# Reordering the hand-written issue lists of a two-layer graph network kernel

## The chip, the cores and the metric

The kernel runs on one core of one Trainium2 chip. Time is device microseconds of one execution, from the runs' own clock; the profile's span counts from the first to the last instruction of one profiled execution. All data are float32, except the masks, which are stored as bfloat16.

## The reference

There are 128 batches of 128 nodes with 512 features, x[128,128,512], and an integer adjacency adj[128,128,128]. Two layers, each with a residual and a normalisation:

```python
# layer 0: attention with 8 heads of 64
q, k, v = x @ Wq + bq, x @ Wk + bk, x @ Wv + bv
logits  = where(adj > 0, q @ k.T / sqrt(64), -1e9)
x = layernorm(x + relu(softmax(logits) @ v @ Wo + bo))
# layer 1: graph attention with one head
Wh = x @ W;  e = leaky(Wh @ a1 [:, None] + Wh @ a2 [None, :])
attention = softmax(where(adj > 0, e, -9e15), axis=1)
x = layernorm(x + leaky(attention @ Wh))
```

## The kernel before, in words

**Engines and order.** Every instruction is issued in an order that is written out. The lists BEGIN, STEADY and PLAN hold short tokens, and a token becomes the few instructions of one piece of work. Each engine (TensorE, VectorE, ScalarE, GpSimd, and SP, which issues the DMAs) works through its own pieces in the order of the list and waits at a piece until what it needs is there. Where pieces of different engines stand relative to each other in a list has no meaning of its own, beyond which buffer a piece is given.

**Stages.** BEGIN is the prologue: it loads and prepares the weights, computes group 0 (a group is four batches) directly, and starts six batches. STEADY has four lists, used for t = 6 to 123 by t % 4. An even t and the odd t after it handle the pair of batches t, t + 1. PLAN is the epilogue for the last four batches.

**Tokens of the steady lists.** `f` and `s` are the first and second batch of the pair: `scores` (TensorE, line 875, eight products of 64 rows, each in two records, into two PSUM banks), `add` (VectorE, line 889: adds the mask, one call for each bank), `reduce` (VectorE, line 898: row maxima), `exp.a.b` (ScalarE, line 909, one call and an accumulator read for each head), `reciprocals` (VectorE, 919), `divide` (ScalarE, 923), `store` and `fetch` (SP: the probabilities go through DRAM, lines 930 and 936, since the fetch reorders them in blocks of 32), `transpose` (VectorE, 942), `attend` (TensorE, 955, products into 64 columns), `copy` (ScalarE, 970), `sum` (GpSimd, 523 to 526).

`h` is a half step of the projections Q, K, V of the next group. They are computed four batches at once with two nested levels of a Strassen-Winograd scheme: seven outer products p1 to p7 (TensorE, line 681, eight records for an even chain, six for an odd one), with partial results in three PSUM banks `st_y`, `st_w`, `st_x`. `a` does the oldest copy out of PSUM that is due (ScalarE, 694), `d` the oldest addition (VectorE, 715), `k` and `k.v` the oldest combination (line 731) on GpSimd and on VectorE. `q` (SP, line 634) fetches the next projection weights into a ring of four tiles. `i.sNx` are the inner sums (line 500) of the next group's inputs, on VectorE with `.v` and else on GpSimd, `m.sum.n` the outer ones (GpSimd).

`z` is the output projection of layer 0 of the pair before, `w` layer 1's product with W: p1 to p7 (TensorE, line 801), t0, t2, t3 (copies, ScalarE, 812), c11 to c22 (VectorE: 1059, 1063, 1047 for z, 1146 for w). A copy t0 or t2 must have read bank y before p6 or p7 adds to it. `z.stats`, `n.stats` (VectorE, 1003 and 1005), `rstd` (GpSimd, 1009 and 1011), `apply` (VectorE, 1024) are the normalisations. `e` is layer 1's attention of one batch (`turn_blocks` 1187, `add` 1191, `maxima` 1197, `exp` 1201, `divide` 1205, `product` 1211, `copy` 1218, all small), `n` its residual (1221) and normalisation, `g` the store and fetch of layer 0's result for layer 1, `v` the round trip of layer 1's row terms, `m` loads, casts and transposes of the inputs.

**Banks.** PSUM has eight banks: three for the projections, five shared by scores, attention outputs and the banks y, w and x of `z` and `w`, `e.product` among them. A piece that asks for a bank waits until the last reader of the tile that held it is done.

Of the kernel before, what the change touches and what calls it, by code (L numbers as in the profile page):

```python
# [23 lines left out]
    y.order.3 y.q.0.0 y.order.2 b0.masks y.q.1.0 y.rows.2 y.rows.3 b4.load.1 b6.load.0  # L24
    b5.load.2 w.bias b2.masks y.q.2.0 y.q.2.1 y.q.1.1 y.oq.1 y.k.3 y.k.1 y.k.2 b4.turn
    b1.cast y.q.3.0 y.q.0.1 b0.cast y.oq.2 b7.load.1 y.q.3.1 b1.mask wk.build.0 b6.turn
    b5.turn wk.build.1 b3.cast b0.mask wk.build.2 wk.build.3 y.ok.2 b2.cast wq.scale.0
    y.oq.0 wq.scale.1 wq.scale.2 y.ok.1 y.ok.3 wq.scale.3 wk.build.4 wk.build.5 y.k.0 y.ok.0
    y.oq.3 s0.scores wk.build.6 b7.turn wk.build.7 b2.mask b3.mask s1.scores g1.0 g1.2
    b9.load.0 b8.load.2 w.halve wq.build.0 wq.build.1 wk.store.0 wq.build.2 s0.add.1  # L30
    s0.add.0 g1.1 i1.s1b b4.masks s0.reduce s1.add.0 s1.add.1 i1.s2b g1.3 wk.store.1
    s0.exp.0.1 s0.exp.6.7 b4.cast s0.exp.4.5 i1.s1a.v wk.store.2 y.v.1 wk.store.3 s0.exp.2.3
    b5.cast q q y.v.0 y.v.2 y.v.3 i1.s3a.v s1.reduce wq.build.4 s0.reciprocals.0
    s0.reciprocals.1 s0.divide.4.5 s0.divide.2.3 i1.s2a wq.build.3 i1.s4a.v wq.build.5
    s1.exp.5.6 s0.divide.0.1 h s1.exp.7 s1.exp.3.4 s0.divide.6.7 y.ov.0 s1.exp.0.1 y.ov.2
# [133 lines left out]
def kernel(  # L169
# [155 lines left out]
    wk = Weights(late)  # L325
# [702 lines left out]
    class LayerZero:  # L1028
# [727 lines left out]
```

## Time and profile before

| | us |
|---|---|
| median of 3 runs | 2305.35 (2304.18 to 2306.50) |
| the profiled execution | 2304.29 |
| its span | 2302.5 |
| granted TensorE clock | 0.998 |

The costliest groups of the page have means of 397 ns for each exponential and each division (ScalarE, 1000 of each), 1189 ns for a row maximum and 1236 ns for the transpose of a batch's probabilities (VectorE, 125 of each), 776 ns for the application of a normalisation (VectorE, 239), and about 275 ns for a projection product and 390 for one of `z` or `w` (TensorE). Matmuls overlap, so these last durations are not what one costs: the distance between two starts is. A "record" is one row of the trace; each float32 product is two of them.

Steady work repeats every four batches: the wait of the second attention product, for example, comes at 1046.67 us and at 1117.08 us, some 70.4 us apart.

### The profile page before, as it was taken

How to read it: one execution, taken by the hardware profiler on the slowest of the kernel's cores; microseconds unless marked ns; L12 is line 12 of the kernel's file. 1: busy time of each engine (PE TensorE's matmuls, PEld its weight loads, DVE VectorE, ACT ScalarE, POOL GpSimd, SP SyncE). 2: the span in 40 equal slices, each digit the busy share in tenths (PEclk: the TensorE clock that was granted, in tenths of full speed). 3: DMA queues.
4: the chain of work that ended last, by engine and by line, in shares of the span. 5: the costliest groups of instructions: out<-in, count | busy, mean ns of one | idle time of the engine just before them, and what ended most of it. 6: DMA issues, size and time to landing. Idle time of an engine off the chain costs nothing.

```text
span 2302.5 us, 52596 instructions
## 1 busy us (share of the span) xinstructions
PE 2265.1 (98%) x17228; PEld 2013.5 (87%) x17228; DVE 2076.6 (90%) x4199; ACT 1661.2 (72%) x5955; POOL 1443.9 (63%) x1723
## 2 busy tenths in 40 slices
PE   9899999999999999999999999999999999999998
PEld 5889888888898898888988988889889889888885
DVE  5889999999999999999999999999999999999977
ACT  3767767777677677776776776877767767768786
POOL 2666676666766666666667666666666676666656
PEclk9999999999999999999999999999999999999999
DMA  9988888878888888888878888788888788888764
GB/s 234 278 232 233 235 236 243 243 233 228 242 234 251 235 230 237 242 243 239 234 228 243 233 246 241 233 233 242 242 240 237 225 246 235 247 236 233 214 214 144
DMA packets 516593, 540.79 MB, mean 235 GB/s; under 512 B 100568, under 2 KB 394336, under 8 KB 516320
## 3 DMA queue, kind: packets, MB, share of 16 engines
q1 hardware_dynamic: 516000, 537.17, 80.3%
q8 instruction: 137, 2.24, 0.4%
q14 instruction: 136, 1.11, 0.2%
q10 hardware_dynamic: 320, 0.26, 0.0%
HBM read 388.96 MB, written 148.31 MB: 233 GB/s over the span
## 4 chain that ended last, share of the span: by engine, by line
PE 58%; DVE 19%; DMA 9%; POOL 6%; SPq 3%; issue 3%; ACT 2%; DVEq 0%; POOLq 0%; ACTq 0%
PE p_y L801 14%; PE st_y L681 13%; PE lg L875 6%; PE p_w L801 6%; PE st_w L681 6%; PE st_x L681 5%; DVE pa L942 4%; PE p_x L801 4%; DMA w_n<-wv 3%; PE p_oT L955 3%; DVE arena L1047 3%; DVE cells L715 2%; DVE st L1003 2%; PE p_h L1211 2%; DVE arena L1024 2%
## 5 line engine op out<-in xcount | busy, mean ns | idle before, releaser
L909 ACT ACTIVATE pa<-pa,nmax 128x128 f32<-128x128 f32 x1000 | 391.6, 397 | 8.7 <-DVE nmax L898 8.7
L923 ACT ACTIVATE pa<-pa,rs 128x128 f32<-128x128 f32 x1000 | 329.2, 397 | 14.4 <-DVE rs L919 14.3
L1009 POOL TENSOR_SCALAR ve<-mv 128x1 f32<-128x1 f32 x256 | 77.6, 303 | 289.5 <-DVE mv L1005 228.4
L694 ACT COPY cells<-st_y 128x384 f32<-128x384 f32 x279 | 131.7, 472 | 101.4 <-PE st_y L681 98.9
L1024 DVE TENSOR_SCALAR arena<-arena,mv,rstd 128x512 f32<-128x512 f32 x239 | 185.5, 776 | 14.3 <-POOL rstd L1011 14.1
L909 ACT ACTIVATION_READ_ACCUMULATOR pa<-pa,nmax 128x1 f32 x1000 | 194.6, 195 | 0.0
L970 ACT ACTIVATE arena<-p_oT,b_cols 128x128 f32<-128x128 f32 x504 | 144.1, 371 | 58.9 <-PE p_oT L955 54.8
L523 POOL TENSOR_TENSOR x1S<-x1T 128x256 f32<-128x256 f32 x62 | 57.6, 929 | 204.2 <-DVE mf L853 204.2
L1011 POOL TENSOR_TENSOR rstd<-ve,mhalf 128x1 f32<-128x1 f32 x256 | 160.8, 628 | 21.3
L1003 DVE BATCH_NORM_STATS2 st<-arena 128x6 f32<-128x512 f32 x248 | 168.0, 678 | 1.2
L889 DVE TENSOR_TENSOR pa<-lg,mf 128x512 f32<-128x512 f32 x250 | 161.2, 675 | 4.6 <-PE lg L875 4.6
L942 DVE STREAM_TRANSPOSE pa<-paz 128x1024 f32<-128x1024 f32 x125 | 154.5, 1236 | 8.5 <-DMA paz<-pa_dram 6.1
L955 PE MATMUL p_oT<-pa,out_V 128*64 128x128 f32 x2000 | 136.9, 279 | 16.8 <-DVE pa L942 16.8
L875 PEld LDWEIGHTS lg<-out_K,out_Q 64*128 64x128 f32 x2048 | 125.0, 188 | 32.4 <-issue 20.4
L875 PE MATMUL lg<-out_K,out_Q 64*128 64x128 f32 x2048 | 149.4, 286 | 0.7 <-ACT out_K L1395 0.7
L694 ACT COPY out_V<-st_y 128x512 f32<-128x512 f32 x124 | 72.1, 581 | 106.7 <-PE st_y L681 106.5
L898 DVE TENSOR_REDUCE nmax<-pa 128x8 f32<-128x1024 f32 x125 | 148.6, 1189 | 0.1
L955 PEld LDWEIGHTS p_oT<-pa,out_V 128*64 128x64 f32 x2000 | 106.7, 136 | 40.0 <-DVE pa L942 31.2
L1218 ACT ACTIVATE arena<-p_h 128x512 f32<-128x512 f32 x120 | 71.5, 596 | 87.8 <-DMA out_dram<-arena 60.5
L801 PE MATMUL p_y<-wo_w,x1S 128*128 128x257 f32 x496 | 134.3, 393 | 0.2
L801 PE MATMUL p_y<-wo_w,x1T 128*128 128x257 f32 x496 | 132.0, 388 | 0.0
L801 PE MATMUL p_y<-wo_w,oS 128*128 128x256 f32 x504 | 129.8, 380 | 0.4 <-ACT y L812 0.4
(301 smaller groups left out, 7851.7 us busy)
## 6 DMA issues: line engine op xcount, KB each, us to landing
paz<-pa_dram SPq DMA_DIRECT2D x504, 128.0 KB, 3.5
pa_dram<-pa SPq DMA_DIRECT2D x125, 512.0 KB, 3.7
w_n<-wk SPq DMA_DIRECT2D x93, 512.0 KB, 5.5
w_n<-wv SPq DMA_DIRECT2D x93, 512.0 KB, 5.1
w_n<-wk SPq DMA_DIRECT2D x93, 384.0 KB, 4.3
w_n<-wv SPq DMA_DIRECT2D x93, 384.0 KB, 5.0
x_dram<-arena SPq DMA_DIRECT2D x128, 256.0 KB, 2.8
xz<-x_dram SPq DMA_DIRECT2D x240, 128.0 KB, 4.1
```

Of the source, the lines that this page charges most:

```text
L681: nc.tensor.matmul(p[:, index, :], lhs, rhs, start=start and index == 0, stop=True, skip_group_check=True,)
L694: nc.scalar.copy(dst, p)
L801: nc.tensor.matmul(p[:, :width], xs()[n][:, kc, :], w[:, PLACE[n], kc, :], start=start and kc == 0, stop=True, skip_group_check=True,)
L875: nc.tensor.matmul(self.lg[r][:, c, :], q[rows, 2 * (b % 2) + c % 2, c // 2, :], k[rows, 2 * (b % 2) + c % 2, c // 2, :], start=c == 0, st ...
L889: nc.vector.tensor_add(by_head[:, r * NC : (r + 1) * NC], self.lg[r].rearrange("p c (b k) -> p c b k", b=4), mf.unsqueeze(1).to_broadcast( ...
L909: nc.scalar.activation(self.pa[:, :, h, :], self.pa[:, :, h, :], AF.Exp, bias=self.nmax[:, h : h + 1], accum_out=self.sums[:, h : h + 1],)
L923: nc.scalar.activation(self.pa[:, :, h, :], self.pa[:, :, h, :], AF.Copy, scale=self.rs[:, h : h + 1])
L942: nc.vector.transpose(self.paT.rearrange("p h (a i) -> p a h i", i=32), self.paz.rearrange("p a (h k) -> p a h k", k=32),)
L955: nc.tensor.matmul(self.oT[r * HD : (r + 1) * HD, c, :], v[:, c % 2, c // 2, r * HD : (r + 1) * HD], self.paT[:, r * NC + c, :], start=c == 0,
L1003: nc.vector.bn_stats(st, self.src)
L1011: nc.gpsimd.tensor_tensor(self.r, ve, mhalf, ALU.pow)
L1024: nc.vector.tensor_scalar(self.src, self.src, self.mv[:, 0:1], self.r, ALU.subtract, ALU.mult)
```

## The change

All three lists are written anew, with the same pieces of work in them. In STEADY:

- `s.scores` follows `f.scores` with no other TensorE piece between them (t % 4 = 0 and 2); before, two half steps and `w.p1`, or `w.p1`, stood there.
- In t % 4 = 1 `z.apply.1` comes behind `s.transpose` and the addition `d` ahead of it (before: `z.apply.1`, `s.transpose`, `z.stats.0`, `d`); `s.add`, `s.exp` and `s.divide` move between lists (`s.exp.5`, `s.exp.6.7`, `s.reciprocals.1`); the `w` products, the half steps, `e` and `n` stand in new orders.
- Inner sums: s1b goes to VectorE, s2b and s3b to GpSimd; of the 24 combinations of a group VectorE does 10 in place of 11.
- SP: `f.fetch` moves from t % 4 = 1 to the end of 0; `q`, `s.store`, `s.fetch` stand at new places.

BEGIN moves `s2.scores` and `s3.scores` forward, has three inner sums of group 1 on GpSimd in place of VectorE (and one the other way), and loads and prepares weights in another order. PLAN puts `s1.scores` behind `s0.scores` and `s3.attend` behind `s2.attend`. One function changes: the norms of a pair are made one at a time.

```diff
 BEGIN = """
...
-    b5.cast q q y.v.0 y.v.2 y.v.3 i1.s3a.v s1.reduce wq.build.4 s0.reciprocals.0
-    s0.reciprocals.1 s0.divide.4.5 s0.divide.2.3 i1.s2a wq.build.3 i1.s4a.v wq.build.5
-    s1.exp.5.6 s0.divide.0.1 h s1.exp.7 s1.exp.3.4 s0.divide.6.7 y.ov.0 s1.exp.0.1 y.ov.2
-    y.ov.1 z0.bw s1.exp.2 b10.load.1 w.w1_load.6 w.load i1.s4b.v a w.w1_load.5 w.w1_load.2
-    w.w1_load.3 q h s2.scores h h i1.s3b.v b4.mask wq.build.7 wq.build.6 y.ov.3 a h q
...
-    d s2.reduce b9.turn d h wv.build.5 s2.exp.6.7 s2.exp.2.3 a s1.divide.2.3 wv.store.0 h
-    s3.scores h s2.exp.0.1 z0.by a h wv.store.2 wv.build.6 wv.build.7 s2.exp.4.5
-    s0.transpose s2.reciprocals.0 b11.turn a s2.divide.2.3 b7.cast d b10.turn h s0.attend
...
+    s1.add.0 s1.add.1 g1.3 i1.s1a i1.s2a i1.s3a wk.store.3 b10.load.1 q q w.load y.v.1
+    s1.reduce i1.s4a s0.reduce wq.build.2 b2.mask w.halve wq.build.3 wq.build.4 b3.mask
+    i1.s1b.v i1.s2b y.v.0 y.v.2 y.v.3 s1.exp.3.4 s0.exp.4.5 y.ov.1 b5.cast s1.exp.7
...
+    z0.by s0.divide.6.7 s0.divide.4.5 y.ov.0 y.ov.3 s2.scores h wv.build.1 wv.build.2 h
...
+    s3.scores h h a s1.divide.6.7 w.w1_load.0 b11.load.2 q h h s0.fetch b10.turn s2.add.0 d
+    s2.reduce d b9.turn b7.cast s2.exp.4.5 s0.transpose b4.mask a s2.exp.0.1 a s2.exp.6.7
+    wv.build.3 wv.build.4 h h s0.attend h h d wv.store.2 wv.store.0 wv.build.5 s1.store
...
 """

 STEADY = {
     0: """
-        k.v n.residual q f.scores h h m.masks m.sum.0 m.sum.1 m.sum.2 m.sum.3 k.v g.apply.0
-        q k.v w.p1 f.add.0 f.add.1 g.store.0 e.turn_blocks a e.add m.cast w.t0 s.scores
-        f.reduce w.p6 f.exp.0.1 f.exp.2.3 d w.t2 f.exp.4.5 f.exp.6.7 d n.stats s.add.0
-        f.reciprocals.0 s.add.1 e.maxima f.reciprocals.1 s.reduce w.p5 h n.rstd w.p7 w.p2 h
-        h m.residuals q g.fetch_both a w.t3 e.exp q q w.c22 w.c11 f.divide.2.3 s.exp.2
-        f.divide.0.1 a f.divide.6.7 e.divide w.p4 w.p3 h h h w.c21 s.exp.5 v.senders
-        f.divide.4.5 s.exp.0.1 a i.s1a.v n.apply d s.exp.6.7 s.exp.3.4 q n.store v.store
-        f.store g.transpose.1 g.transpose.0 i.s3a.v e.product h m.x_pair i.s2a i.s1b m.turn
-        d k.v m.mask i.s3b.v a s.reciprocals.0 s.reciprocals.1 w.c12 d i.s2b.v k.v e.copy
-        v.fetch
+        f.scores m.sum.0 m.sum.2 e.turn_blocks k.v m.sum.1 k.v g.apply.0 n.residual f.add.1
+        f.add.0 s.scores q w.p1 h e.add f.reduce n.stats s.add.0 a w.t0 w.p6 h w.p2 m.turn d
+        e.maxima s.add.1 f.exp.2.3 w.t2 f.exp.0.1 f.exp.6.7 a f.exp.4.5 e.exp w.p7 h m.sum.3
+        s.reduce d h h f.reciprocals.0 e.divide i.s1a.v w.p5 g.store.0 m.residuals m.masks q
+        q n.rstd g.fetch_both w.t3 m.cast a f.divide.2.3 a f.divide.0.1 s.exp.0.1 q d w.c22
+        w.c11 f.reciprocals.1 w.p4 w.c21 v.senders f.divide.6.7 h w.p3 h h n.apply i.s1b.v
+        k.v g.transpose.1 m.mask g.transpose.0 n.store v.store f.divide.4.5 a s.exp.2
+        s.exp.3.4 s.exp.5 i.s2a f.store m.x_pair v.fetch f.fetch e.product h i.s2b a d
+        i.s3a.v s.reciprocals.0 w.c12 d e.copy k i.s3b
     """,
     1: """
-        p.sum.0 z.by n.residual h z.p2 h k h a s.divide.5.6 i.s4a a f.fetch z.p1 h h d
-        n.stats n.rstd k.v m.turn e.turn_blocks s.divide.3.4 s.divide.7 s.divide.0.1
-        s.divide.2 n.apply z.bw z.t0 h z.p6 z.t2 a m.cast z.p5 z.p7 k k k h z.c11
-        f.transpose z.t3 e.add d z.p4 s.store z.c22 a z.p3 h h m.mask e.maxima z.c21 s.fetch
-        n.store q e.exp a a d z.stats.1 e.divide i.s4b h e.product h f.attend z.c12 e.copy
-        f.copy p.sum.1 z.rstd.1 p.sum.2 z.apply.1 s.transpose q z.stats.0 d s.attend s.copy
-        p.sum.3 z.rstd.0 k k s.sum.2 s.sum.0 s.sum.1 k s.sum.3 m.x_one z.store.1
+        z.by s.divide.2 k.v n.residual h h h z.p1 i.s4b i.s4a a s.exp.6.7 z.t0 z.p2 z.p6 d
+        n.stats s.reciprocals.1 a s.divide.0.1 s.divide.3.4 s.divide.7 s.divide.5.6 k.v
+        e.turn_blocks m.turn z.c11 h h h s.store z.t2 e.add z.bw a e.maxima e.exp d
+        f.transpose n.rstd z.p5 z.p7 h q m.x_one s.fetch z.t3 e.divide z.c22 a m.cast z.p4
+        z.c21 n.apply n.store k h h z.p3 m.mask d h z.stats.1 z.c12 q k p.sum.0 k z.rstd.1
+        e.product h d f.attend a a e.copy q s.transpose s.attend z.stats.0 z.apply.1 f.copy
+        s.copy p.sum.2 k k p.sum.1 z.rstd.0 s.sum.0 p.sum.3 k z.store.1 s.sum.2 s.sum.1
+        s.sum.3
     """,
     2: """
-        f.scores n.residual g.apply.0 w.p1 f.add.1 f.add.0 s.scores e.turn_blocks w.t0 e.add
-        w.p6 f.reduce w.t2 w.p2 h w.p7 m.turn k.v k.v f.exp.4.5 f.exp.6.7 f.exp.0.1 k.v w.p5
-        h w.t3 a f.exp.2.3 n.stats f.reciprocals.1 w.c22 e.maxima w.c11 f.reciprocals.0
-        e.exp f.divide.2.3 n.rstd w.p4 h w.c21 v.senders a d n.apply f.divide.4.5
-        f.divide.6.7 f.divide.0.1 e.divide s.add.0 s.add.1 d h w.p3 q g.store.0 m.residuals
-        m.masks h e.product h h a a g.fetch_both m.x_one n.store v.store s.reduce
-        g.transpose.0 w.c12 q f.store v.fetch q m.cast d g.transpose.1 m.mask s.exp.5 e.copy
+        n.residual e.turn_blocks f.scores g.apply.0 f.add.0 f.add.1 s.scores w.p1 e.add w.t0
+        w.p2 w.p6 w.p5 f.reduce e.maxima k f.exp.4.5 e.exp w.t2 w.p7 f.exp.6.7 f.exp.2.3
+        w.t3 m.residuals g.store.0 q m.masks f.exp.0.1 h a h m.turn k.v n.stats e.divide
+        f.reciprocals.1 k.v m.x_one g.fetch_both s.add.1 f.divide.6.7 w.p4 n.rstd w.c21 h
+        n.apply d w.c11 m.cast h w.c22 f.reciprocals.0 v.senders a d e.product h h n.store
+        f.divide.0.1 s.add.0 w.p3 h a f.divide.4.5 s.reduce a f.divide.2.3 v.store q f.store
+        v.fetch e.copy w.c12 g.transpose.1 g.transpose.0 d m.mask
     """,
     3: """
-        s.exp.3.4 z.by s.exp.6.7 k.v n.residual n.stats p.sum.0 h f.fetch a s.exp.2 z.p2
-        z.p1 h h s.exp.0.1 z.t0 n.rstd q k.v z.p6 p.sum.1 p.sum.2 s.reciprocals.0
-        s.reciprocals.1 d s.divide.5.6 a s.divide.0.1 s.divide.7 s.divide.3.4 h
-        e.turn_blocks n.apply d z.t2 s.divide.2 m.cast m.turn h a a h z.p7 h h d m.mask
-        z.c11 z.bw e.add a z.t3 k k k e.maxima f.transpose k z.p5 q e.exp h h z.p4 h a a d
-        z.c22 s.store q q e.divide z.c21 s.fetch z.p3 h d z.stats.1 z.c12 k h n.store
-        e.product z.rstd.1 p.sum.3 z.apply.1 d z.stats.0 h h f.attend s.transpose a e.copy a
-        s.attend f.copy s.copy k z.rstd.0 s.sum.0 q z.store.1 s.sum.2 s.sum.1 m.x_one
-        s.sum.3
+        z.bw p.sum.2 s.exp.2 z.by h z.p1 q s.exp.5 s.exp.6.7 a z.t0 s.exp.0.1 s.exp.3.4 h h
+        z.p6 n.residual n.stats m.turn d s.reciprocals.0 e.turn_blocks s.reciprocals.1 a k
+        p.sum.0 n.rstd k d z.t2 e.add s.divide.3.4 z.p2 h z.p5 h z.c11 s.divide.7 e.maxima
+        s.divide.5.6 s.divide.0.1 s.divide.2 k.v n.apply h m.cast a p.sum.1 z.p7 f.fetch h h
+        a z.t3 e.exp m.x_one q q d f.transpose e.divide z.c22 k k.v a z.p4 h h s.store z.p3
+        h a a k.v k q q h d z.c21 d z.stats.1 h a z.c12 p.sum.3 z.rstd.1 d e.product h h k
+        m.mask z.apply.1 z.stats.0 s.fetch n.store q q s.transpose f.attend s.attend f.copy
+        e.copy s.copy k z.rstd.0 s.sum.2 s.sum.0 s.sum.1 s.sum.3 z.store.1
     """,
 }
 
 PLAN = """
-    m2.adj e0.sender s0.scores b0.p1 v.p6 m2.cast v.p5 s0.add.0 s0.add.1 b0.t0 a0.by v.t2
-    s1.scores v.p7 v.p2 s0.reduce s0.exp.4.5 s0.exp.0.1 s0.exp.6.7 el.residual s0.exp.2.3
-    s1.add.1 m2.mask s1.add.0 s0.reciprocals.1 s0.reciprocals.0 s0.divide.4.5 s1.reduce
-    al.apply.0 s2.scores a0.p1 b0.p2 s0.divide.2.3 al.fetch.1.0 b0.p6 al.store.0 m3.adj u.p1
...
-    s1.divide.6.7 v.c21 a0.bw a0.t2 u.p7 s3.scores a0.p7 u.p5 s1.divide.0.1 b0.t2
...
-    s1.attend s0.attend s2.fetch s0.copy b1.c22 e0.divide a0.c12 e1.divide s1.copy s3.store
...
-    s2.attend a0.apply.1 b1.c21 a0.apply.0 a1.t2 a1.bw e2.exp a0.store.1 a0.store.0 x2.x
-    a1.p7 e3.turn a1.p5 s2.copy e3.add a1.t3 s3.transpose e2.divide e3.maxima s1.sum.3
-    e0.rstd e1.rstd s3.attend a1.c22 a1.p3 e4.sender e3.exp s3.copy a2.by e0.apply a1.p4
...
+    m2.adj s0.scores s1.scores e0.sender e0.turn el.residual s0.add.0 s0.add.1 s0.reduce
+    v.p6 a0.by e0.add m2.cast x0.x b0.p2 v.p5 s1.add.0 s1.add.1 al.apply.0 s1.reduce
+    e0.maxima v.t2 v.p2 b0.p1 al.store.0 v.p7 s0.exp.0.1 s0.exp.4.5 s0.exp.6.7 s0.exp.2.3
+    a0.p1 u.p1 al.fetch.1.0 m3.adj x1.x v.c11 m2.mask s0.reciprocals.0 s1.exp.4.5 s1.exp.6.7
+    s1.exp.2.3 u.t0 a0.t0 s0.divide.2.3 b0.t0 s1.exp.0.1 s2.scores s2.add.1 v.t3
+    s0.reciprocals.1 s2.add.0 b0.c11 s1.reciprocals.1 s1.reciprocals.0 s2.reduce u.p6 a0.p6
+    s3.scores b0.p6 u.t2 s0.divide.6.7 e1.sender a0.t2 s0.divide.4.5 m3.cast b0.t2
...
+    a1.by e0.exp b1.t3 e2.sender e1.exp e1.divide s1.attend s0.attend s3.store b1.p4
...
+    x2.x a0.store.1 s2.attend s3.attend e2.exp e3.exp a1.t3 s2.copy e1.apply e0.stats a1.c22
...
 """
...
         def stats(self, h):
-            self.norms = self.norms or [
-                Norm(X1[2 * self.pair + n], self.on_scalar) for n in range(2)
-            ]
+            self.norms = self.norms or {}
+            self.norms[h] = Norm(X1[2 * self.pair + h], self.on_scalar)
             self.norms[h].stats()
```

## The prediction, made before the result was seen

> **What bounds the kernel now.** I read four views in this order: the page's busy line, the busy time by three stretches, the list of waits, and the order in time around one hand-over between two pairs of batches.
>
> ```profile
> PE 2265.1 (98%) x17228; PEld 2013.5 (87%) x17228; DVE 2076.6 (90%) x4199; ACT 1661.2 (72%) x5955; POOL 1443.9 (63%) x1723
> 0.00:150.00 150.00, 137.46 (x910) 109.08 (x911) 112.58 (x218) 86.79 (x308) 76.16 (x77) 1.00 0.88 247
> 150.00:2150.00 2000.00, 1986.87 (x15399) 1787.28 (x15399) 1840.24 (x3714) 1461.59 (x5267) 1278.50 (x1505) 1.00 0.82 238
> 2150.00:2302.50 152.50, 140.76 (x923) 117.19 (x921) 123.81 (x269) 112.77 (x383) 89.27 (x143) 0.98 0.57 181
> ```
> Columns of the last three: stretch, length, then busy time of PE, weight loads, VectorE, ScalarE, GpSimd, clock, DMA share, GB/s. TensorE is the bound. In the middle 2000 us it is idle for 13.1 us, in the first 150 for 12.5, in the last 152.5 for 11.7, of which some 8 us are the tail behind its last product. VectorE, with 1840 of 2000 us, is close behind: it has 8% to give before it becomes the bound.
>
> ```profile
> PE p_oT L955 <- DVE pa L942: 16.8, 60, 2.0
> ```
> The one wait that comes back every pair (total, times, longest): the attention product of the second batch waits for VectorE's transpose of its probabilities. In the middle stretch it is all of the 13.1 us idle.
>
> ```profile
> 1045.33 1.09 PE L955 MATMUL p_oT<-pa,out_V 128*64 128x128 f32 x16
> 1046.67 1.09 PE L955 MATMUL p_oT<-pa,out_V 128*64 128x128 f32 x16 [0.25 <-DVE pa L942]
> 1047.69 1.16 PE L875 MATMUL lg<-out_K,out_Q 64*128 64x128 f32 x16
> 1048.79 1.14 PE L801 MATMUL p_y<-wo_w,x1T 128*128 128x257 f32 x4
> 1049.85 1.16 PE L875 MATMUL lg<-out_K,out_Q 64*128 64x128 f32 x16
> 1050.94 1.14 PE L801 MATMUL p_y<-wo_w,x1S 128*128 128x257 f32 x4
> 1051.92 1.03 PE L801 MATMUL p_x<-wo_w,x1T 128*128 128x257 f32 x4
> 1052.79 0.38 PE L681 MATMUL st_y<-xS,wq 128*128 128x128 f32 x2
> ...
> 37.64 2.06 PE L875 MATMUL lg<-out_K,out_Q 64*128 64x128 f32 x32 [0.68 <-ACT out_K L1395]
> 39.62 3.70 PE L1401 MATMUL st_w<-arena,xT 128*128 128x512 f32 x8
> ```
> Start, duration, what; the difference of two starts is what a group really costs. Four records of p_x cost 0.87 us (1051.92 to 1052.79), but p_y between the two scores costs 1.06, and p_y behind the second 0.98. A score run of 16 records costs 1.10 and 1.09, yet two batches in one run, which the prologue already has, cost 1.98 for 32. So TensorE pays, inside what the page calls busy, for each change between whole-array products and the 64-row scores.
>
> **The change, part by part.**
>
> *Scores of two batches in one run.* Pieces of today's order: 1.10 + 1.06 + 1.09 + 0.98 = 4.23 us for score, p1, score, next product. In the new lists for t%4 = 0 and 2 no TensorE piece stands between f.scores and s.scores: 1.98 + 0.98 + 0.87 = 3.83. That is 0.40 us a pair, with nothing else changed. Pairs t = 6 to 123 are 59: 23.6 us. In PLAN the four scores go from four runs to three, and the four attention products from three runs to two: 2 x 0.40 = 0.8. BEGIN has as many changes of kind before as after. **Sum: -24.4 us.** It is on TensorE's own time, so no cover is needed; it is lost only where a new wait stands in the place.
>
> *The wait before the second attention product.* VectorE's order before its transpose (L942) in t%4 = 1 was, behind TensorE's p3: mask, maxima, c21, a cell addition, stats 1, divide, c12, apply 1, transpose. The last are these rows:
>
> ```profile
> 1043.45 0.42 DVE L1059 TENSOR_TENSOR y<-p_w,y 128x256 f32<-128x256 f32 x1
> 1043.90 0.69 DVE L1047 SCALAR_TENSOR_TENSOR arena<-y,arena 128x512 f32<-128x512 f32 x1
> 1044.51 0.95 DVE L1024 TENSOR_SCALAR arena<-arena,mv,rstd 128x512 f32<-128x512 f32 x1
> 1045.38 1.23 DVE L942 STREAM_TRANSPOSE pa<-paz 128x1024 f32<-128x1024 f32 x1
> ...
> 1056.86 0.54 DVE L1024 TENSOR_SCALAR arena<-arena,mv,rstd 128x512 f32<-128x512 f32 x1
> ```
> The new list puts apply 1 (0.87 from start to start) behind the transpose. From p3's end TensorE there has 0.90 (a half step of 8 L681 records, 0.112 apart) + 0.87 (e.product) + 0.67 + 1.10 = 3.5 us until the second product; VectorE has c12 (0.45 + 0.61), a cell addition 0.60 and the transpose 1.17 = 2.8. So in t%4 = 1 the wait should go. In t%4 = 3 apply 1 and stats 0 stay ahead of the transpose; there I see no clear gain. Bounds: 0 and -20 (16.8 idle, or 1.34 minus about 1.0 for the first product, times 59). I take the half that t%4 = 1 has: **-8 us**.
>
> *Pieces between VectorE and GpSimd.* Per four batches one s1b comes to VectorE; s2b, s3b and one k go to GpSimd. VectorE: 0.47 - 0.63 - 0.47 - 0.60 = -1.2 us of some 65 (1840 x 70.4 / 2000); GpSimd +2.3 of 45. Neither is the bound: 0. Their cover is VectorE's 8%. The apply shows what keeping apart may bring: 0.95 while GpSimd runs a tensor_tensor, 0.54 while it is idle (1056.86), 239 of them with mean 0.776 on the page, so up to 239 x 0.24 = 57 us of VectorE's time. But the score additions are not slowed: in the same view two take 1.27 at 1049.37 with GpSimd busy beside them, and 0.68 is what one takes alone at 1057.70. So the relief is VectorE's, and reaches the end only through the transposes above and the softmax start below.
>
> The Trainium skill speaks against counting on more (SBUF — State Buffer, section "Who interferes with whom"): a lost race for the shared port pair blocks the loser for the whole instruction, it isn't a split of bandwidth. By that rule a collision with a 1.27 us GpSimd piece could cost an apply up to 1.27, not the 0.41 of the row, and the 57 us could be three times as much; the row decides, and on VectorE's slack both are worth nothing to the end.
>
> *What is queued behind a new wait.* With both scores in one run TensorE comes 0.4 + 0.3 us sooner to the products that need the softmax's start. In t%4 = 2 the new ScalarE order is e.add, w.t0, f.exp.4.5, e.exp, w.t2; w.t2 (and TensorE's w.p7, which needs it) now stands behind two exponentials that wait for f.reduce; before, w.t2 stood ahead of them. From the start of the second attention product TensorE needs 1.0 + 1.98 + 0.98 + 3 x 0.87 = 6.6 us to w.p7. VectorE from the same point: stats 0.77, apply 0.45 to 0.87, residual 0.60, turn 0.23, apply 0.45 to 0.87, additions 1.20, reduce 1.09 = 4.8 to 5.6; ScalarE then 2 x 0.39 + 0.40 + 0.27 = 1.5 and two hand-overs of about 0.1: 6.5 to 7.3. The wait is 0 to 0.7 us, once in four batches, 30 times: 0 to 21. Five PSUM banks also have to serve 2 attention outputs, 4 scores and p1 in a row; ScalarE's two copies of 1.0 us (1046.47, 1047.81) end before the third bank is asked for again, about 2.3 us into a run that needs it at 3.0. In t%4 = 0 ScalarE copies f, e (0.5), s, still in time. I take **+4 us** of 0 to 30, as VectorE has slack from the transposed apply in just this step.
>
> *DMA order.* The fetches of f's probabilities move from t%4 = 1 into 0, s.store and s.fetch earlier in 1, behind two weight fetches in 3. There s.store can issue about 8 us into the step, the page's 3.7 and 3.5 us to land make 16, and the transpose is due at 18 to 19: cover of 2 us, and then a loss one for one. 0, in the bounds above.
>
> *New prologue and epilogue.* Same pieces. Idle there: 12.5 and 11.7 - 8 = 3.7 us. s2.scores now fills the place where TensorE waited at 53 us for ScalarE's copies, and three inner sums leave VectorE ahead of the first transpose (one comes); s0.attend comes two half steps (1.3 us) earlier, which may cost as much. Bounds -12 and +10; I take **-2**.
>
> **Sum** against the profiled execution, which took 2304.29 (span 2302.5): 2304.3 - 24.4 - 8 - 2 + 4 = 2273.9. The median of the runs shown, 2305.35, lies 1.06 above it: **2275 us**.
>
> **Rivals.**
>
> *The full gain* (12%): all attention waits and most of the prologue's go: 2305.4 - 24.4 - 18 - 8 = 2255. For it: the wait list has nothing else. Against it: t%4 = 3 keeps its order before the transpose.
>
> *Half given back* (14%): w.t2 waits its 0.7 us 30 times (+21) while the transposes gain 8 and the ends 2: 2305.4 - 24.4 - 8 - 2 + 21 = 2292.
>
> *Slower* (18%): the softmax start becomes the bound. TensorE now reaches the second half of the w products before VectorE has reduced the first scores, in t%4 = 2 (w.t2 and Q1.t2 behind the exponentials) and in t%4 = 0 (five VectorE operations, 2.5 us, stand before f.add; w.t2 and V4.t3 stand behind exponentials). At 1.4 us per four batches over 29.5 groups that is +41, and 2305.4 - 24.4 + 41 = 2322. It decides from 24.4 / 29.5 = 0.83 us per four batches. For it: VectorE is 92% busy in the middle, and stretches of 0.4 us by GpSimd come when its sums run. Against it: VectorE's load falls by 1.2 us.
>
> *No effect* (4%): other waits fill exactly the room of the removed changes, 2305. TensorE's 0.40 us a pair is its own time, so only chance would bring this.
>
> **How the numbers follow.** Forecast 52%, own range 2262 to 2289; full gain 12%, half given back 14%, slower 18%, no effect 4%. What a measurement of this kernel can tell from no change is about 0.2% (4.6 us). Faster 0.78, same 0.04, slower 0.18. The range leaves out the slower half of the slow case and the best of the full gain: 2252 to 2310.
>
> **What would show it.** The scores stand as x32 in the order in time, costing 1.98, with no 1.06 group between; the wait of p_oT for pa falls to half or less; ScalarE-caused idle time of p_y and st_y products stays under 10 us in the middle stretch. The forecast is wrong if p_y L801 waits for ScalarE's t2 (L812) or st_y for its copies (L694) tens of times, or if p_oT waits as long as before.

## The result, and the profile after

| | before | after |
|---|---|---|
| median | 2305.68 us (2304.18 to 2308.91, 14 runs) | 2298.43 us (2294.51 to 2308.77, 14 runs) |
| ratio, with its 95% interval | | 0.9971 [0.9961, 0.998] |
| span of the profiled execution | 2302.5 | 2296.6 |

Faster by 7 us (0.3%); the forecast was 30. The three stretches of the kernel after (columns as in the prediction: stretch, length, busy time of PE, weight loads, VectorE, ScalarE, GpSimd, clock, DMA share, GB/s):

```profile
0.00:150.00 150.00, 134.88 (x874) 106.18 (x875) 108.61 (x205) 81.00 (x286) 76.66 (x76) 0.98 0.84 238
150.00:2150.00 2000.00, 1980.54 (x15457) 1793.14 (x15456) 1813.95 (x3674) 1462.06 (x5299) 1377.51 (x1565) 1.00 0.81 239
2150.00:2296.60 146.60, 134.77 (x900) 113.03 (x899) 119.15 (x261) 110.21 (x373) 91.02 (x143) 0.98 0.59 187
```

TensorE is busy for 6 us less of the middle 2000 than before while it gets 58 more records done; so it saves time and then stands idle for more of it. VectorE is 26 us less busy, GpSimd 99 us more.

The order in time around the hand-over of two pairs, TensorE of the kernel after:

```profile
1046.94 0.39 PE L680 MATMUL st_w<-xS,wq 128*128 128x128 f32 x2
1047.26 1.97 PE L954 MATMUL p_oT<-pa,out_V 128*64 128x128 f32 x32
1049.16 2.06 PE L874 MATMUL lg<-out_K,out_Q 64*128 64x128 f32 x32
1051.14 1.14 PE L800 MATMUL p_y<-wo_w,x1T 128*128 128x257 f32 x4
1052.12 1.03 PE L800 MATMUL p_x<-wo_w,x1T 128*128 128x257 f32 x4
1052.98 1.03 PE L800 MATMUL p_y<-wo_w,x1S 128*128 128x257 f32 x4
1053.86 1.03 PE L800 MATMUL p_w<-wo_w,x1S 128*128 128x257 f32 x4
1055.01 1.14 PE L800 MATMUL p_y<-wo_w,x1S 128*128 128x257 f32 x4
```

Both gains that the forecast named are there. The scores are one run of 32 and cost 1.98 us (1049.16 to 1051.14). The attention products are one run too, 1.90 us where they cost 2.36 before (1045.33 to 1047.69). But the last line, `w.p7`, starts 1.15 us behind the one before it, where such a product costs 0.87: it waits 0.28 for ScalarE's `w.t2`. The list of waits of the middle stretch (total, times, longest) has more such places:

```profile
PEld p_y L800 <- ACT arena L811: 15.9, 28, 0.9
PEld st_y L680 <- DVE out_K L714: 14.4, 17, 0.9
...
PE st_y L680 <- DVE out_K L714: 7.6, 17, 0.5
...
PEld st_w L680 <- DVE out_V L714: 5.3, 20, 0.3
...
PE st_y L680 <- DVE cells L714: 2.3, 5, 0.5
...
PE p_oT L954 <- DVE pa L941: 1.4, 5, 0.4
```

PEld is the weight load; it waits ahead of the product. The attention wait is down from 13 us and 57 times to 1.4 and 5. The six chains of a group's projections, in order, are called Q0, Q1, K2, K3, V4 and V5 here. In place of the attention wait stand `w.p7` for ScalarE's copy (28 times, t % 4 = 2), K3's p1 for VectorE's addition to K2 (17, t % 4 = 3), V4's st_w for an addition to V4 (20, t % 4 = 0) and, in the Q0 that follows, a few for V5's cells.

**Where the time went, from start to start.** From the first score record of t = 6 to the first of the epilogue each kernel has 15,977 TensorE records. I took the distance of each start from the one before, in the one profile of each kernel. For a record of 128, 256 or 512 columns it is 0.112, 0.216 or 0.429 us; what lies over 0.13 us above that is a wait, and the next record then costs some 0.1 more, which I count with it. In us:

| steady part | products, scores, changes of kind | pairs of attention products | waits and the 0.1 behind them | sum |
|---|---|---|---|---|
| before | 1949.7 | 128.3 | 2.1 | 2080.1 |
| after | 1924.8 | 105.2 | 40.9 | 2071.0 |
| difference | -24.9 | -23.1 | +38.8 | -9.1 |

The prologue up to t = 6 took 136.1 us (before 130.6) and the rest 89.6 (91.8), so +5.5 and -2.2: with -9.1 that is the 5.9 us between the two spans.

### The profile page after: what moved, and what is told of

It reads as the page before. It is cut to its first block, busy times and chain, and to the rows that moved or that the text cites. A ratio compares the mean times of both kernels' runs of the same rounds, so it can differ in the third digit from the quotient of the medians.

```text
span 2296.6 us, 52699 instructions
## 1 busy us (share of the span) xinstructions
PE 2250.2 (98%) x17228; PEld 2012.4 (88%) x17228; DVE 2041.7 (89%) x4138; ACT 1653.3 (72%) x5955; POOL 1545.2 (67%) x1784
## 4 chain that ended last, share of the span: by engine, by line
PE 57%; DVE 18%; POOL 8%; DMA 8%; ACT 4%; issue 3%; SPq 2%; DVEq 0%; POOLq 0%; ACTq 0%
PE st_y L680 18%; PE p_y L800 12%; PE st_w L680 8%; PE p_w L800 7%; PE st_x L680 4%; DVE pa L888 3%; DVE nmax L897 3%; PE p_h L1209 2%; DMA paz<-pa_dram 2%; POOL rstd L1010 2%; POOL out_K L730 2%; PE p_x L800 2%; POOL out_Q L730 2%; ACT pa L908 2%; DMA xz<-x_dram 2%
## 5 line engine op out<-in xcount | busy, mean ns | idle before, releaser
L524 POOL TENSOR_TENSOR x1S<-x1T 128x256 f32<-128x256 f32 x62 | 48.6, 783 | 245.7 <-PE st_y L680 245.7
L1010 POOL TENSOR_TENSOR rstd<-ve,mhalf 128x1 f32<-128x1 f32 x256 | 192.8, 753 | 21.3
L1008 POOL TENSOR_SCALAR ve<-mv 128x1 f32<-128x1 f32 x256 | 84.9, 332 | 132.6 <-DVE mv L1004 130.9
L714 DVE TENSOR_TENSOR cells<-st_w,cells 128x384 f32<-128x384 f32 (+1 forms) x217 | 123.1, 567 | 42.4 <-ACT cells L693 40.6
L1023 DVE TENSOR_SCALAR arena<-arena,mv,rstd 128x512 f32<-128x512 f32 x239 | 143.6, 601 | 17.3 <-POOL rstd L1010 17.3
L897 DVE TENSOR_REDUCE nmax<-pa 128x8 f32<-128x1024 f32 x125 | 152.3, 1219 | 4.2
L730 POOL TENSOR_TENSOR out_Q<-out_Q,cells 128x512 f32<-128x512 f32 x93 | 130.8, 1406 | 17.0 <-DVE out_Q L730 11.8
L954 PE MATMUL p_oT<-pa,out_V 128*64 128x128 f32 x2000 | 126.9, 278 | 7.3 <-DVE pa L941 7.2
L874 PE MATMUL lg<-out_K,out_Q 64*128 64x128 f32 x2048 | 132.8, 279 | 0.7 <-ACT out_K L1393 0.7
L800 PE MATMUL p_y<-wo_w,arena 128*128 128x256 f32 x504 | 130.8, 382 | 0.6 <-ACT pr_t L811 0.6
L730 POOL TENSOR_TENSOR out_K<-out_K 128x512 f32<-128x512 f32 x32 | 53.7, 1679 | 113.2 <-PE st_x L680 103.6
## 6 DMA issues: line engine op xcount, KB each, us to landing
paz<-pa_dram SPq DMA_DIRECT2D x504, 128.0 KB, 3.5
xz<-x_dram SPq DMA_DIRECT2D x240, 128.0 KB, 3.3
```

Source lines behind the costliest of these rows:

```text
L730: (by or engine).tensor_add(*(t(n) for t, n in (dst, left, right)))
L800: nc.tensor.matmul(p[:, :width], xs()[n][:, kc, :], w[:, PLACE[n], kc, :], start=start and kc == 0, stop=True, skip_group_check=True,)
L874: nc.tensor.matmul(self.lg[r][:, c, :], q[rows, 2 * (b % 2) + c % 2, c // 2, :], k[rows, 2 * (b % 2) + c % 2, c // 2, :], start=c == 0, st ...
L897: nc.vector.tensor_reduce(self.nmax, by_head, AX.XY, ALU.max, negate=True)
L1010: nc.gpsimd.tensor_tensor(self.r, ve, mhalf, ALU.pow)
L1023: nc.vector.tensor_scalar(self.src, self.src, self.mv[:, 0:1], self.r, ALU.subtract, ALU.mult)
```

## The experiments

Line numbers are those of the kernel that an experiment starts from: 680, 693, 714, 730, 800, 811, 874, 908, 941 and 954 of the kernel after are 681, 694, 715, 731, 801, 812, 875, 909, 942 and 955 before; 1219 is 1221. Every run on the kernel before also makes the norms of a pair one at a time, as the change does; in a1_merge, which leaves the attention order alone, the account's attention column stays at 128.0 with it (before 128.3). "Steady part" is the stretch just defined, of the profiled execution. The kernel before took 2305.8 to 2307.9 us beside these runs.

**a1_merge: the second score product beside w.p1, on the kernel before.**

```diff
 0: """
-        q k.v w.p1 f.add.0 f.add.1 g.store.0 e.turn_blocks a e.add m.cast w.t0 s.scores
+        q k.v s.scores w.p1 f.add.0 f.add.1 g.store.0 e.turn_blocks a e.add m.cast w.t0
...
 2: """
-        f.scores n.residual g.apply.0 w.p1 f.add.1 f.add.0 s.scores e.turn_blocks w.t0 e.add
+        f.scores n.residual g.apply.0 s.scores w.p1 f.add.1 f.add.0 e.turn_blocks w.t0 e.add
```

> The kernel before, with nothing changed but the place of the second score product: in t%4 = 0 and 2 it stands beside the first, ahead of w.p1. My theory (the merge is worth the 0.40 us a pair that the forecast gave it, and what ate it in the changed kernel are waits that its other moves made): 2305.7 - 23.6 = 2282, up to 2290 where TensorE, 0.7 us sooner, now waits for the softmax start; the attention products go on waiting some 15 us or more. Rival A (VectorE sets the pace, so that whatever TensorE saves comes back as a wait whatever the order): 2298 or more. Rival B (the 0.40 us is no cost of the change of kind but was there for another reason): 2305, with the score run of 32 records costing 2.2 to 2.4 us.

2339.93 us, 1.0139 [1.0124, 1.0153]: slower by 32, within Rival A's bound alone. TensorE's waits in the middle stretch:

```profile
PE p_y L801 <- ACT arena L812: 28.6, 56, 0.6
PE p_oT L955 <- DVE pa L942: 12.5, 55, 0.5
```

The product behind `w.p1` needs ScalarE's `w.t0`, and the second score run had covered that copy; without it TensorE stands there every pair. The changed kernel has `w.p2` or a half step in that place. In t % 4 = 0 two half steps still lie between the scores, so this run undoes a cover more than it tries the merge. It does settle Rival B: the runs of 32 that it makes in t % 4 = 2 cost 1.98 us, not 2.2 to 2.4.

**a2_steady: the new steady lists between the old prologue and epilogue.**

> The changed kernel's four steady lists between the prologue and the epilogue of the kernel before. My theory (the gain was lost in the steady part; the new ends are worth some 3 us either way): 2295 to 2302 against 2298.4 of the changed kernel. Rival C (the new prologue or epilogue ate it, with its waits of 3.5 and 1.6 us before the first attention products): 2290 or less.

2301.34 us, 0.9971 [0.9958, 0.9985], the same ratio as the change itself. The gain and its loss are both in the steady lists.

**a3_t2 and b2_t2mid: w.t2 sooner, on the kernel after.**

```diff
 2: """
-        w.p2 w.p6 w.p5 f.reduce e.maxima k f.exp.4.5 e.exp w.t2 w.p7
+        w.p2 w.p6 w.t2 w.p5 f.reduce e.maxima k f.exp.4.5 e.exp w.p7
```

> The changed kernel with one token moved: in t%4 = 2 w.t2 stands ahead of f.exp.4.5 and e.exp in ScalarE's order, as it did before. My theory (w.p7 waits 28 times in the middle stretch, 9.1 us, only for this order, and some 3 us more of short gaps behind it): 2298.4 - 9 to - 12 = 2286 to 2290. Rival A (VectorE sets the pace): the wait only moves to the next product that needs the softmax, 2296 to 2299.

2315.11 us, 1.0035 [1.0023, 1.0047]: 17 us slower than the change, which neither reading had. ScalarE and TensorE of this kernel:

```profile
1272.36 0.37 ACT L811 COPY arena<-p_y 128x257 f32<-128x257 f32 x1 [1.45 <-PE p_y L800]
1274.10 0.37 ACT L811 COPY arena<-p_y 128x257 f32<-128x257 f32 x1 [1.37 <-PE p_y L800]
1274.37 0.40 ACT L908 ACTIVATE pa<-pa,nmax 128x128 f32<-128x128 f32 x1
```

```profile
1277.48 1.14 PE L800 MATMUL p_y<-wo_w,x1T 128*128 128x257 f32 x4 [0.35 <-ACT arena L811]
```

ScalarE stands 1.37 us at `w.t2` until TensorE has done `w.p6`, and the exponentials behind it start 5.17 us after the start of the scores instead of 4.28. `w.t3` is late in turn, and `w.p4` waits 0.51 us 28 times. The order that the forecast blamed was the better one of the two.

```diff
 2: """
-        f.exp.4.5 e.exp w.t2 w.p7
+        f.exp.4.5 w.t2 e.exp w.p7
```

> The changed kernel with w.t2 between f.exp.4.5 and e.exp in t%4 = 2. In a3_t2, ahead of both, it made ScalarE wait for w.p6 and held the exponentials 0.9 us, and the wait went to w.p4 (0.51 us, 28 times). Between them it waits for nothing: w.p6 is done when f.exp.4.5 is. My theory: w.p7's 28 waits of 0.28 and the 0.1 behind each go, e.exp is 0.35 later and nobody waits for that: 2298.4 - 7 to - 11 = 2287 to 2291. Rival A: 2296 or more, the wait turning up at w.p4 or at the bank of K3.p1.

2300.39 us, 0.997 [0.9958, 0.9982]: nothing gained. `w.p7` does not wait any more (2 times); K3's p1 waits 24 times in place of 17, and Q1's p4 has 28 new waits of 0.15. Rival A.

**a4_mend and b3_mend2: several additions sooner, on the kernel after.**

```diff
 3: """
-        n.residual n.stats m.turn d
+        d n.residual n.stats m.turn
 0: """
-        m.sum.3 s.reduce d
+        m.sum.3 d s.reduce
-        m.mask g.transpose.0
+        m.mask d g.transpose.0
```

> The same token, and three of VectorE's order: the addition that frees the bank of K3.p1 (d for K2.c11) ahead of residual, stats and turn in t%4 = 3, the one that frees V4.p4's bank (d for V4.c22) ahead of s.reduce in t%4 = 0, and d for V5.c11 ahead of the second transpose of g in t%4 = 0. In the changed kernel these four waits are 28, 17, 20 and 5 of the middle stretch, 27 us, and 36 with the short gaps behind them. My theory: 2298.4 - 20 to - 30 = 2268 to 2278. Rival A: most of it comes back as later waits, 2290 or more.

The kernel also has a3_t2's move of `w.t2`, and the `d` ahead of `i.s3a.v` in list 0 is the one that moves up to the transposes.

2334.53 us, 1.0116 [1.0103, 1.0129]: 36 us above the change and 19 above a3_t2. `w.p4` waits as in a3_t2 (28 times, 9.7 us). K3's p1 waits no longer, but ahead of the residual VectorE itself waits 1.0 us for TensorE at the addition (28 times), and a later half step waits for ScalarE's copy (27 times, 12.1 us). That the one brings the other is read from the order, not shown alone. A mend that makes the other engine wait is none.

b3_mend2 has the middle place for `w.t2`, the last two lines above for V5's addition, the swap of b4_race below, and these:

```diff
 3: """
-        n.residual n.stats m.turn d
+        n.residual n.stats d m.turn
 0: """
-        f.reduce n.stats s.add.0
+        f.reduce s.add.0
...
-        s.reduce d h h
+        s.reduce d n.stats h h
```

> The changed kernel with five small moves: w.t2 as in b2_t2mid; the addition for K2.c11 between stats and turn in t%4 = 3 (a4_mend had it ahead of the residual, where VectorE waited 1.0 us for TensorE); n.stats behind the addition for V4.c22 in t%4 = 0; the addition for V5.c11 one transpose sooner; and p.sum.0 ahead of GpSimd's addition of Q1 in t%4 = 3. My theory: the waits of the changed kernel, 36 us, go for the most part and no queue waits for a thing that is not done: 2270 to 2280. Rival A: 2290 or more.

2298.92 us, 0.996 [0.9947, 0.9973]: as the change, and Rival A. V4's wait, 9.2 us behind the start of the scores, is gone, but 28 waits of 0.42 stand 18.1 us behind it, for VectorE's cells.

**b4_race: one swap on GpSimd, on the kernel after.**

```diff
 3: """
-        a k p.sum.0 n.rstd k
+        a p.sum.0 k n.rstd k
```

> The changed kernel with one swap on GpSimd in t%4 = 3: p.sum.0 ahead of the addition of Q1's first block. In the changed kernel that addition (1.27 us) starts within 0.1 us of VectorE's residual, which takes 1.81 us instead of 0.68 in 17 of 28 cases, the same in which K3.p1 waits 0.61. Theory (the two engines race for the same thing and the loser stands still for the whole of the other's instruction): with a GpSimd piece of 0.73 in that place the residual takes at most 1.4, K3.p1's wait goes or falls below 0.1 in most cases: 2298.4 - 8 to - 13 = 2285 to 2290. Rival: the residual waits for something else (its data), and both its 1.81 us and the wait stay: 2298.

2290.63 us, 0.9932 [0.9917, 0.9946]: 8 us off the change, just under the 8 to 13 that the theory gave. The reason, all engines of the kernel after, in two groups of batches at the same place:

```profile
1277.11 1.27 POOL L730 TENSOR_TENSOR out_Q<-out_Q,cells 128x512 f32<-128x512 f32 x1
1277.12 1.81 DVE L1219 TENSOR_TENSOR arena<-arena 128x512 f32<-128x512 f32 x1
...
1347.30 1.83 POOL L730 TENSOR_TENSOR out_Q<-out_Q,cells 128x512 f32<-128x512 f32 x1
1347.32 0.68 DVE L1219 TENSOR_TENSOR arena<-arena 128x512 f32<-128x512 f32 x1
```

One of the two takes its own time (0.68 or 1.27), the other its own and some 1.13 or 0.56 more. In the first group VectorE lost, and K3's p1 stood still; in the second it won, and nothing waited:

```profile
1279.74 1.03 PE L800 MATMUL p_x<-wo_w,arena 128*128 128x256 f32 x4
1281.21 0.49 PE L680 MATMUL st_y<-xT,w_n 128*128 128x128 f32 x2 [0.45 <-DVE out_K L714]
...
1349.94 1.03 PE L800 MATMUL p_x<-wo_w,arena 128*128 128x256 f32 x4
1350.80 0.39 PE L680 MATMUL st_y<-xT,w_n 128*128 128x128 f32 x2
```

With a GpSimd piece of 0.73 us in that place VectorE's residual still loses 18 times, but takes some 1.26 and not 1.81, and K3's waits fall from 10.3 us to 1.2. In b4_race:

```profile
1267.03 0.74 POOL L522 TENSOR_TENSOR x1S<-x1T 128x256 f32<-128x256 f32 x1
1267.04 1.27 DVE L1219 TENSOR_TENSOR arena<-arena 128x512 f32<-128x512 f32 x1
```

**c1_m35: that swap, and n.stats behind V4's addition.**

```diff
 0: """
-        f.reduce n.stats s.add.0
+        f.reduce s.add.0
...
-        s.reduce d h h
+        s.reduce d n.stats h h
```

> b4_race's swap on GpSimd, and n.stats behind the addition for V4.c22 in t%4 = 0, without the other three moves of b3_mend2. In b3_mend2 that second move took away the wait at V4's st_w 8.9 us into the pair; what came in its place (27 waits of 0.42 at Q0's st_w, 17.4 us in) goes by my reading back to the addition for V5.c11, put ahead of a transpose, where VectorE waits for TensorE. My theory: b4_race's 2290.6 less the 16 waits of 0.24 + 0.1: 2284 to 2288. Rival A (each wait taken away only comes back): 2290 or more.

2286.25 us, 0.9914 [0.9901, 0.9928]: as expected, 12 us off the change with two tokens moved.

**b1_merge2 and c2_merge: the merge with a cover for w.t0, on the kernel before.** b1_merge2 reads the second batch's K before its last additions, so its 2394.1 us belong to another computation and say nothing.

```diff
 0: """
-        f.scores h h
+        f.scores s.scores w.p1 h h
...
 2: """
-        f.scores n.residual g.apply.0 w.p1
+        f.scores n.residual g.apply.0 s.scores w.p1 w.p2
```

> The kernel before with its two score products really side by side in both lists and with cover for w.t0 behind w.p1: in t%4 = 0 f.scores, s.scores, w.p1 and then the two half steps; in t%4 = 2 f.scores, s.scores, w.p1, w.p2. (In a1_merge w.p6 stood right behind w.p1 and waited 0.67 us for ScalarE's w.t0 56 times, and in t%4 = 0 two half steps still stood between the scores.) My theory (the merge is worth 0.40 us a pair; the period per four batches falls from 70.46 to 69.66 but for new waits of at most 0.4): 2282 to 2294. Rival A (what TensorE saves comes back as waits on ScalarE's and VectorE's orders): 2300 or more.

In c2_merge the additions to K come first, and `n.residual` and `g.apply.0` stand later:

```diff
 0: """
-        k.v n.residual q f.scores h h m.masks m.sum.0 m.sum.1 m.sum.2 m.sum.3 k.v g.apply.0
-        q k.v w.p1 f.add.0 f.add.1 g.store.0 e.turn_blocks a e.add m.cast w.t0 s.scores
+        k.v k.v q f.scores m.masks m.sum.0 m.sum.1 m.sum.2 k.v s.scores w.p1 h h m.sum.3
+        g.apply.0 n.residual q f.add.0 f.add.1 g.store.0 e.turn_blocks a e.add m.cast w.t0
...
 2: """
-        f.scores n.residual g.apply.0 w.p1 f.add.1 f.add.0 s.scores e.turn_blocks w.t0 e.add
-        w.p6 f.reduce w.t2 w.p2 h w.p7
+        f.scores n.residual g.apply.0 s.scores w.p1 w.p2 f.add.1 f.add.0 e.turn_blocks w.t0
+        e.add w.p6 f.reduce w.t2 h w.p7
```

> The kernel before with the merge alone, this time with the additions to K that the second scores need ahead of them (b1_merge2 read K before them, so its time means nothing): in t%4 = 0 k.v, k.v, k.v, then s.scores beside f.scores, w.p1, the two half steps; in t%4 = 2 f.scores, s.scores, w.p1, w.p2. My theory (0.40 us a pair): 2305.7 - 23.6 = 2282, up to 2295 where the second scores wait for those additions. Rival A (what TensorE saves comes back as waits on the other engines' orders): 2300 or more; then the merge needs an order of VectorE and ScalarE of its own, and its gain is no number that stands alone.

2356.1 us, 1.0218 [1.0204, 1.0232]: slower by 50. One wait of 1.6 us in every group, at the first `w` product on x1S behind the half steps in t % 4 = 0, makes 45 us in the middle stretch. That is Rival A's reading; neither run got the merge alone out of the old orders. In the other list, t % 4 = 2, no wait over 0.17 us comes back behind c2_merge's scores; that half by itself was not run.

**c3_apply: apply 1 back ahead of the transpose in t % 4 = 1, on the kernel after.**

```diff
 1: """
-        q s.transpose s.attend z.stats.0 z.apply.1 f.copy
+        q z.apply.1 s.transpose s.attend z.stats.0 f.copy
```

> The changed kernel with apply 1 back ahead of s.transpose in t%4 = 1, as before. In the changed kernel two attention products cost 1.69 to 1.81 us from the first to the last record, before 2.13 and 2.17, in both kinds of pair, though t%4 = 3 keeps apply 1 ahead of the transpose. Forecast's theory (the order of apply 1 takes the wait away): every other pair gets 0.4 back, 28 x 0.4 = +11, 2306 to 2312. Rival (it is GpSimd's pieces out of VectorE's way, apply now 0.54 instead of 0.95): the wait comes back by 0.1 or less, 2298 to 2302.

2300.3 us, 0.9975 [0.9964, 0.9987]. The attention products of every other pair cost 2.02 again instead of 1.69, yet the time moves by 2 us at most: `w.p7`'s waits shrink from 9.1 to 2.9 us. Half of each theory: the order does take the wait away, and it is worth nothing here.

**c4_split: the merge undone, on the kernel after.**

```diff
 0: """
-        s.scores q w.p1
+        q w.p1 s.scores
...
 2: """
-        s.scores w.p1
+        w.p1 s.scores
```

> The changed kernel with the score products apart again: w.p1 between them in both lists, all else as it is. My theory: +23.6 for 59 merges undone, less the waits that this 0.4 us covers (w.p7's 0.28 + 0.1 in every other pair, 11 us, and up to 5 of V4's): 2305 to 2314. Rival A (the merge's gain had all gone into waits): 2296 to 2301.

2300.1 us, 0.9967 [0.9955, 0.9979]; Rival A. Its steady part is 2071.0 us, that of the change; that they agree to a tenth is luck. In the account: products and changes of kind 1947.8 (+23.0), attention 107.6 (+2.4), waits 15.6 (-25.3).

**d1_softmax, d2_softmax_split, d3_m35_split: is the merge worth more with fewer waits?** d1 is c1_m35 with one of VectorE's operations out of the chain from the scores to `w.t2`; d2 and d3 undo the merge in d1 and in c1, with c4_split's edit.

```diff
 2: """
-        f.scores g.apply.0 f.add.0 f.add.1
+        f.scores f.add.0 f.add.1
...
-        f.reduce e.maxima k
+        f.reduce e.maxima g.apply.0 k
```

> c1_m35 (2286.3) with g.apply.0 behind e.maxima in t%4 = 2, so that VectorE's 0.54 us for it no longer stands between the scores and f.reduce. In c1_m35 w.p7 still waits 28 times 0.30, with 0.1 behind each, for ScalarE's w.t2, which stands behind f.exp.4.5 and e.exp. Theory S (in this place the chain f.add, f.reduce, f.exp, w.t2 sets the pace): that wait goes, 11 us, and little comes back: 2275 to 2280. Rival A (each wait only moves on): 2284 or more.

> d1_softmax with the score products apart again (w.p1 between them in both lists). Theory S: with no wait behind them the merge is worth what TensorE saves, 59 x 0.40: 18 to 24 us above d1_softmax. Rival A: 8 us or less above it, as in c4_split (2 us).

> c1_m35 with the score products apart again. In c1_m35 w.p7's 28 waits of 0.40 (11 us) are left to cover the 0.40 us, in every other pair only. Theory S: half of the merge counts, 8 to 14 us: 2294 to 2300. Rival A: 2286 to 2289.

d1: 2288.18 us, 0.992 [0.9902, 0.9937]. No wait of `w.p7` is left, and nothing is gained over c1: 15 waits, 8.3 us in all, stand at a `z` product that none was at before, and the attention column is 4.8 us longer. Rival A. d2: 2296.61, 0.9959 [0.9944, 0.9974], 8 us above d1. d3: 2295.34, 0.9948 [0.9936, 0.996], 9 us above c1. So where the race is mended, 8 to 9 us of the merge's 25 reach the end; d2 came out at the bound of Rival A, d3 within Theory S. The account of d3 against c1 shows where the rest goes: products and changes of kind +23.7 without the merge, waits -14.4 (21.0 to 6.6), steady part +9.4. d2 against d1 is +2.9 there, as d1's profiled execution is one of its longer ones (2293.14).

**d4_apply and e1_apply2: the transposes alone, on the kernel before.**

```diff
 1: """
-        p.sum.2 z.apply.1 s.transpose q z.stats.0 d s.attend
+        p.sum.2 s.transpose q z.stats.0 z.apply.1 d s.attend
```

> The kernel before with apply 1 behind s.transpose in t%4 = 1, and nothing else: the forecast's step of -8 by itself. In the changed kernel this order was worth 0.33 us at the attention products of every other pair (c3_apply). Theory S (the kernel before has no other wait, so TensorE and this one wait set its pace): 28 x 0.33 = 9 off: 2295 to 2299. Rival A: 2303 or more.

2293.58 us, 0.9942 [0.993, 0.9955]: one token is worth 14 us, twice the whole change. TensorE of this kernel in t % 4 = 1, and its only two waits in the middle stretch:

```profile
1043.85 0.39 PE L681 MATMUL st_w<-xS,wq 128*128 128x128 f32 x2
1044.17 1.97 PE L955 MATMUL p_oT<-pa,out_V 128*64 128x128 f32 x32
1046.06 1.16 PE L875 MATMUL lg<-out_K,out_Q 64*128 64x128 f32 x16
```

```profile
PE p_oT L955 <- DVE pa L942: 5.9, 29, 0.5
PE st_w L681 <- ACT cells L694: 0.7, 1, 0.7
```

The two products cost 1.89 here and 2.36 before: 0.47 us for an idle time that the profile gave as 0.25. The other 0.22 lies on both sides of the gap: before, the first product stretches over 1.09 us (1.34 less the 0.25) and the second over 1.02 from start to start, and in one run each has half of 1.89, 0.95. 29 x 0.47 = 13.6, and the account's attention column falls by 13.8 (128.3 to 114.5) with no other column moving by more than 0.3. The 29 waits left are those of t % 4 = 3.

```diff
 3: """
-        p.sum.3 z.apply.1 d z.stats.0 h h f.attend s.transpose a
+        p.sum.3 d z.stats.0 h h f.attend s.transpose z.apply.1 a
```

> d4_apply (2293.6) with apply 1 behind s.transpose in t%4 = 3 as well. There VectorE waits 0.46 us for GpSimd's rstd ahead of apply 1, which then takes 0.94, all ahead of the transpose. In d4_apply these pairs still cost 2.11 from the first to the last record of the attention products, the other 1.69. Theory S: 28 x 0.42 = 12 off: 2280 to 2284. Rival A: the later apply holds the additions to K and the first scores of t%4 = 0, 2288 or more.

2284.98 us, 0.9907 [0.9892, 0.9922], just above its bound of 2284 (the kernel before was at 2307.65 beside it). Its stretch in the middle:

```profile
150.00:2150.00 2000.00, 1995.86 (x15530) 1805.28 (x15529) 1828.52 (x3746) 1471.16 (x5326) 1299.81 (x1518) 1.00 0.83 240
```

TensorE is idle for 4 of 2000 us. With two tokens moved the steady part is 2059.4, where the change reached 2071.0. This and c1_m35 (2057.8) are the fastest here; their intervals overlap.

**e2_ends: the new prologue and epilogue on that.**

> e1_apply2 with the changed kernel's prologue and epilogue. The forecast had these at -2 (-12 to +10); a2_steady gave -3 with a steady part that was 2.5 us better, so -3 to -5: 2276 to 2280. Rival C: the 3.5 us wait before the first attention product in the new prologue counts, 0 to +5 against e1_apply2.

2290.41 us, 0.9924 [0.9911, 0.9937]: 5 us above e1_apply2, with a steady part 0.5 us longer. The expected gain is not there; Rival C's 0 to +5 is nearer. The intervals of the two overlap, so this doesn't settle a size. Over the profiled executions, b1_merge2 left out, the prologue up to t = 6 took 133.3 us on average with the old list (130.6 to 135.3, 6 kernels) and 135.3 with the new one (132.1 to 139.7, 13 kernels), the rest 90.7 and 89.9: together about +1.

## Why the prediction was wrong

- **Scores in one run, -24.4.** The size was right, 24.9 in the account. What the prediction said beside it, "on TensorE's own time, so no cover is needed; it is lost only where a new wait stands in the place", named the way it went: undone in the changed kernel it is worth nothing (c4_split), since 25 us of waits stood in the place. But "no cover is needed" did not hold: in c1_m35 against d3_m35_split the merge takes 23.7 us off TensorE's own time and brings 14.4 us of waits for the other engines.
- **The attention wait, -8.** 23.1 in the account, mis-sized twice. The pair of t % 4 = 1 was priced by its idle time, 0.28 us, and cost 0.47, since some 0.2 more is lost around the gap (d4_apply); it gave 13.4 of the 23.1. And t % 4 = 3, "no clear gain", gave the other 9.7. There, in all 30 pairs, apply 1 takes 0.54 us in the changed kernel and waits for nothing, where it waited 0.45 for rstd and took 0.94; that this is the cause is read from the rows, no run has it alone.
- **New waits, +4 of 0 to 30: the step that failed.** They are 38.8, more than the whole gain that was forecast. The one mechanism priced was there: `w.p7` behind `w.t2`, 28 times, 9.1 us and 2.9 behind, inside its own bounds of 0 to 21. But it was the only one priced. The sum has no term for the moment when VectorE's additions free the three banks of the projections, and most of the other waits stand there: 12.1 us at K3, 6.8 at V4 and some 5 behind V5. The remaining 5 or so stand elsewhere, 3.0 of them at a shared bank to whose scores VectorE has yet to add the mask. Of all these, 2.1 us were there before.
- **Pieces between VectorE and GpSimd, 0.** The prediction set the rule of the Trainium skill (SBUF — State Buffer, section "Who interferes with whom"), that a lost race blocks the loser for the whole instruction, against a row of 0.41 us, and said that on VectorE's slack both are worth nothing. The residual's 1.81 us for 0.68 agrees with the rule, and the 17 races lost in the middle stretch are K3's 17 waits; b4_race's one swap brought 8 us back. A mean of 8% slack says nothing of one bank's: with the residual 1.13 us longer K3's p1 waits 0.61, with it 0.58 longer 0.07, so by both there was room for about 0.5.
- **Prologue and epilogue, -2.** About +1, in the bounds.
- **The rivals.** "Half given back" had 2292 and the right kind of cause, with one place for five; "no effect", at 4%, had other waits fill the room that is won, which is nearer to what the account shows. What would show the forecast wrong was met: `p_y` waits for ScalarE's `t2` 28 times.

What holds the pace once these waits stand is not settled. Four edits that each took a wait away or gave one back (b2_t2mid, c3_apply, c4_split, d1_softmax) moved the time by 2 us or less, which fits several chains of nearly one length better than one (d1 loosened one and another was there), but no run shows it. What is shown is the other side: on the kernel before, where TensorE has hardly another wait, an edit counts in full (d4_apply, 13.8 of 13.8); on the kernel after, 25 us of its own time counted for nothing (c4_split).

## What to carry to other kernels

Before a saving on the bound engine is put in a sum, list every bank or buffer that this engine will now ask for sooner, and who frees it: here, with the next engine 92% busy, 38.8 of 48 us came back as waits. Try a large reorder's parts alone on the old order, too; here one token in each of two lists beat the whole of it. And price a stall by the distance from start to start, not by the idle time beside it.

## What was not expected of the hardware

GpSimd's addition starts 7 to 18 ns ahead of VectorE's residual in all 29 cases of the changed kernel where these two meet, by the recorded starts. VectorE loses 18 of them (1.80 to 1.81 us) and wins 11 (0.68, GpSimd then 1.82 to 1.84): the recorded order doesn't tell who wins. The changed kernel's runs spread over 14 us (2294.5 to 2308.8), those of the kernel before over 5; races that fall otherwise in each execution may be why, but one profile of each kernel doesn't show it, and b4_race, where this race costs half as much, spreads over 14 us too.
